# An attention and graph-convolution kernel: scores and values in double blocks, half products summed in PSUM

## The chip, the cores and the metric

The kernel runs on one core of a Trainium2 chip. The metric is the device time of one execution in microseconds (us). Before the change the median of three runs is 2770.14 us (2769.64 to 2770.96).

## What is computed

`x` is 32 batches of 512 nodes by 512 features, `adj` a 512 x 512 adjacency matrix. Two layers, each with residual and layer norm, all in float32:

```python
def _L0_gnn_ref(x, adj, Wq, bq, Wk, bk, Wv, bv):   # H, HD = 8, 64
    q = (x @ Wq + bq).reshape(b, n, H, HD)          # k, v alike
    scores = jnp.einsum('bihd,bjhd->bhij', q, k) / jnp.sqrt(jnp.float32(HD))
    mask = jnp.where(adj == 0, jnp.float32(-1000000000.0), jnp.float32(0.0))
    weights = jax.nn.softmax(scores + mask[None, None, :, :], axis=-1)
    return jnp.einsum('bhij,bjhd->bihd', weights, v).reshape(b, n, H * HD)
...
x = _layernorm(x + _L0_gnn_ref(x, adj, ...), axis=-1)
x = _layernorm(x + _L1_gnn_ref(x, adj, weight, bias), axis=-1)   # norm_adj @ (x @ weight) + bias
```

## The kernel before

All work is in `unshifted` (L50). A second function, `general`, runs only if a test at the end finds inputs out of range; it does not run here. `InOrder` (L36) records every operation of PE, DVE, ACT and POOL in program order, so each engine's queue is the order in which the code calls it, and all operations carry one line number, L44. Operations are told apart by their tiles' names.

**Products by seven.** The four matrix products with weights (values, keys, queries, and the second product of the convolution) are block products of 2 x 2 blocks done with seven multiplications instead of eight. `seven` (L309) plays them as seven pieces. A piece is four matmuls of 128 x 256 columns, each two instructions on PE, into a fresh PSUM bank; DVE, ACT and POOL add the products up in SBUF (tiles `e1`, `u1`, `u2`). `values_of` (L343) makes V, `keys_and_queries` (L368) makes K and Q for two of four head pairs, `second` in `convolve` (L710) the last product. XT, the transposed x, and the weights are held as seven half blocks, of which three are sums or differences.

**Attention.** The 8 heads go in four pairs `g`, in the order 0, 2, 1, 3; a block is one batch and one pair. `scores` (L402) computes, for two of four node tiles, keys by queries of two heads at once in the two row halves of the array (`sc`, 64 rows), DVE adds the mask (`e<-sc,maskT`), ACT takes the exponential. `accumulate` (L420) sums the exponentials on POOL, `fold` (L482) transposes and reduces these sums on DVE. `values` (L439) multiplies V by the exponentials, two heads in the two column halves of the array (`av`). `unload_values` (L456) transposes `av` on DVE into `yb`, and four DMAs on SP's queue scatter `yb` into `yT`.

**After attention.** `finish` (L532) divides by the sums, adds the residual `xr` (POOL), norms, and splits the result into two float32r parts `hi` and `lo`. `convolve` (L666) multiplies them by the adjacency (`first`, eight matmuls per tile into `zT`), then by the weights (`second`), and norms again; `store` (ACT) and a DMA put the result out.

**PSUM.** Eight banks: three pairs (`wide`), one bank `narrow`, one `av`. Pieces take wide, wide, wide, narrow in turn; scores take the pairs (L95 to L103).

**The order.** The loop at L864 goes through the 128 blocks. In one step it issues scores of block k and values of block k-1, each in halves of two tiles; in the middle part (`double`, L929) two such steps stand together, so that PE sees scores, values, scores, values, 16 instructions each, and then a share of other work: products for batch b+1, the rest of attention and the convolution for batch b-1. The shares are lists (`beside`, `side`, `cut`) written out by hand, which say after which piece of PE work each small operation of DVE, ACT and POOL is issued. `put_off` delays the POOL sums among them. The last three blocks and the end have an order of their own.

Of the kernel before, what the change touches and what calls it, by code (L numbers as in the profile page):

```python
# [49 lines left out]
def unshifted(  # L50
# [14 lines left out]

# [4 lines left out]
    G = H // 2  # L83
    SCALE = 1.0 / HD**0.5
    tensor, vector, scalar, gpsimd = (InOrder(tc, e) for e in (nc.tensor, nc.vector, nc.scalar, nc.gpsimd))
# [4 lines left out]
    small = ctx.enter_context(tc.tile_pool(name="small", bufs=3))  # L90

    psum = ctx.enter_context(tc.tile_pool(name="psum", bufs=1, space=bass.MemoryType.PSUM))
    WIDE = dict(tag="wide", bufs=3)  # L95
    turn_of = {"n": 0, "order": (WIDE, WIDE, WIDE, dict(tag="narrow"))}

    def bank(shape, tags=None):
        if tags is None:
            order = turn_of["order"]  # L100
            tags = order[turn_of["n"] % len(order)]
            turn_of["n"] += 1
        return psum.tile(shape, F32, name="mm", **tags)  # L103

    HALF = N // 2
# [3 lines left out]
    def load_x(b, j):  # L115


        if b == 1 and j == 1:
            X[b, j] = work.tile([P, 8, DT, 32], F32, name="x1", tag="e", bufs=6)
        else:  # L120
            X[b, j] = acts.tile([P, 8, DT, 32], F32, name="x", bufs=1)
        for q in range(4):
            nc.sync.dma_start(
                X[b, j][32 * q : 32 * (q + 1)],
                x[b, ts(j, HALF), ts(q, P)].rearrange("(k s) (t r) -> s k t r", s=32, r=32),
            )
# [12 lines left out]

# [9 lines left out]

# [10 lines left out]

    def combine(b, at):
        to, a, c = ((4, 2, 0), (5, 3, 4), (6, 3, 2), (2, 5, 1))[at]
        engine = gpsimd if b else vector
        engine.tensor_tensor(XT[:, to], XT[:, a], XT[:, c], ALU.subtract)
# [3 lines left out]
    def load_residual(b):  # L168

        if b < B - 2:  # L170
            t = acts.tile([P, NT, D], F32, name="xr", tag="zT", bufs=1)
            R[b] = [t[:, i, :] for i in range(NT)]
        elif b == B - 2:
            t = [acts.tile([P, 2, D], F32, name="xr2", tag=tag, bufs=n) for tag, n in (("x", 1), ("kq", 5))]
            R[b] = [t[i // 2][:, i % 2, :] for i in range(NT)]
        else:
            R[b] = [wk[:, i].rearrange("p u o -> p (u o)") for i in range(NT)]
        for i in range(NT):
            nc.sync.dma_start(R[b][i], x[b, ts(i, P), :])

# [55 lines left out]
    if B > 1:  # L236
        load_x(1, 0)
        load_x(1, 1)
# [19 lines left out]

    FINE = consts.tile([P, B + 2 * NT], F32, name="fine")
    dis = consts.tile([P, NT], F32, name="dis")  # L260

    plainT = acts.tile([P, NT, N], F32, name="plainT", tag="hi", bufs=1)

    def adjacency(m):


        p = bank([P, N])
        for n in range(NT):
            tensor.transpose(p[:, ts(n, P)], adj_sb[:, n, ts(m, P)], ident)
        vector.tensor_scalar(maskT[:, m, :], p, 0.0, FAR, op0=ALU.is_equal, op1=ALU.mult)  # L270
        scalar.copy(adjT[:, m, :], p)
        scalar.copy(plainT[:, m, :], p)

    def compare(m):

# [9 lines left out]

# [9 lines left out]

    KQ, V = {}, {}
    bias = consts.tile([P, 2, DT], F32, name="bias")
    step = consts.tile([P, 2, 2], F32, name="step")

    def biases():  # L300
        vector.tensor_copy(bias[:, 0], bk_c)
        vector.tensor_scalar(bias[:, 1], bq_c, SCALE, None, op0=ALU.mult)
        vector.tensor_sub(step, bias[:, :, 2:], bias[:, :, :2])

    def value_biases():

        vector.tensor_sub(bv_r[:, HALF:], bv_r[:, HALF:], bv_r[:, :HALF])

    def seven(multiply, first, middle, out, early=False):  # L309


        t = {}

        def piece(k, i, j):
            p = bank([P, 2, HALF])
            multiply(p, i, j)
            if k == 0:
                t["e1"] = work.tile([P, 2, HALF], F32, name="e1", bufs=1)
                first(t["e1"], p)
            elif k == 1:  # L320
                vector.tensor_add(out(0, 0), t["e1"], p)
            elif k == 2:
                t["u1"] = t["e1"]
                vector.tensor_add(t["u1"], t["e1"], p)
            elif k == 3:
                t["u2"] = work.tile([P, 2, HALF], F32, name="u2", bufs=1)
                middle(t["u2"], t["u1"], p)
                if early:
                    vector.tensor_add(out(1, 0), t["u2"], out(1, 0))
            elif k == 4:  # L330
                vector.tensor_add(out(1, 1), t["u2"], p)
                vector.tensor_add(t["u1"], t["u1"], p)
            elif k == 5 and early:
                scalar.activation(out(1, 0), p, AF.Copy, scale=-1.0)
            elif k == 5:
                vector.tensor_sub(out(1, 0), t["u2"], p)
            elif k == 6:
                vector.tensor_add(out(0, 1), t["u1"], p)

        order = [(0, 0), (1, 1), (5, 5), (6, 6), (4, 4), (3, 2), (2, 3)]  # L340
        return [(2.1, piece, (k, *order[k])) for k in ((0, 1, 5, 2, 3, 4, 6) if early else range(7))]

    def values_of(b):  # L343


        def multiply(p, i, j):
            for r in range(2):
                for u in range(2):
                    tensor.matmul(
                        p[:, r, :], XT[:, j, u, ts(r, P)], wv[:, i, u, :],  # L350
                        start=u == 0, stop=u == 1,
                    )

        def first(e1, p):
            V[b] = acts.tile([P, NT, D], F32, name="v")
            vector.tensor_add(e1, p, bv_r[:, None, :HALF].to_broadcast([P, 2, HALF]))

        def middle(u2, u1, p):
            vector.tensor_add(u2, u1, p)
            engine = gpsimd if b > 1 else vector  # L360
            engine.tensor_add(u2, u2, bv_r[:, None, HALF:].to_broadcast([P, 2, HALF]))

        def out(i, j):
            return V[b][:, 2 * j : 2 * j + 2, ts(i, HALF)]

        return seven(multiply, first, middle, out, b == 0)

    def keys_and_queries(b, r):  # L368


        def multiply(p, i, j):
            for c, w in enumerate((wk, wq)):
                for u in range(2):
                    tensor.matmul(
                        p[:, c, :], w[:, i, u, ts(r, P)], XT[:, j, u, :],
                        start=u == 0, stop=u == 1,
                    )

        def first(e1, p):
            for g in (r, r + 2):  # L380
                KQ[b, g] = acts.tile([P, 2, N], F32, name="kq", bufs=5)
            for c in range(2):
                scalar.activation(e1[:, c], p[:, c], AF.Identity, bias=bias[:, c, r : r + 1], scale=1.0)

        def middle(u2, u1, p):
            for c in range(2):
                vector.scalar_tensor_tensor(
                    u2[:, c], u1[:, c], step[:, c, r : r + 1], p[:, c], op0=ALU.add, op1=ALU.add
                )

        def out(i, j):
            return KQ[b, r + 2 * i][:, :, ts(j, HALF)]

        return seven(multiply, first, middle, out)

    def turns(b):

        return [(0, turn, (b, 0))], [(0, turn, (b, 1))] + [(0, combine, (b, k)) for k in range(4)]
# [3 lines left out]
    def scores(s, between=()):  # L402

        b, g, jj = s
        E[s] = [work.tile([P, 2, N], F32, name="e", bufs=6) for _ in range(2)]
        for l in range(2):
            j = 2 * jj + l
            e = E[s][l]
            p = psum.tile([P, 2, N], F32, name="sc", **WIDE)
# [7 lines left out]
            run(between)  # L417
            between = ()

    def accumulate(s, ls=(0, 1)):  # L420


        b, g, jj = s
        n = 2 * ORDER.index(g) + jj
        a = None
        if b == B - 1:
            if n > 1:
                t, at = ((wq, 0), (wq, 2), (wq, 4), (wk, 4), (wv, 4), (XT, 4))[n - 2]
                a = t[:, at : at + 2].rearrange("p k u o -> p k (u o)")
        if a is None and (jj == 0 or b == B - 1):  # L430
            a = work.tile([P, 2, N], F32, name="acc", bufs=2)
        if a is not None:
            ACC.setdefault((b, g), []).append(a)
            gpsimd.tensor_add(a, E[s][0], E[s][1])
        else:
            for l in ls:
                gpsimd.tensor_add(ACC[b, g][0], ACC[b, g][0], E[s][l])

    def values(s, later=False):  # L439

        b, g, jj = s
        e = E.pop(s)
        if jj == 0:
            AV[b, g] = psum.tile([P, N], F32, name="av")
        av = AV[b, g]
        for l in range(2):
            j = 2 * jj + l
            for k in range(2):
                tensor.matmul(
                    av[k * HD : (k + 1) * HD, :], V[b][:, j, ts(2 * g + k, HD)], e[l][:, k, :],  # L450
                    start=j == 0, stop=j == NT - 1,
                )
        if jj and not later:
            unload_values(b, g)

    def unload_values(b, g):  # L456
        av = AV[b, g]
        if (b, g) == blocks[-1]:
            turned = work.tile([P, N], F32, name="avT", tag="yb", bufs=1)
            scalar.copy(turned[:, :HALF], av[:, :HALF])  # L460
            vector.tensor_copy(turned[:, HALF:], av[:, HALF:])
            AV[b, g] = turned
            return

        yb = work.tile([P, 4, NT, 32], F32, name="yb", bufs=1)
# [817 lines left out]
```

## Time and profile before

| What | us |
|---|---|
| median of three runs | 2770.14 |
| the profiled execution, its own time | 2769.45 |
| its span, first to last instruction | 2767.6 |
| first matmul starts | 4.69 |
| first scores start | 50.07 |
| one batch in the middle (its pattern repeats) | 85.20 |
| last product of the tail starts | 2752.49 |

The page of the profile gives, for each engine, the time it is busy in the span: PE is the matmul engine, PEld its weight loads, which overlap, DVE the vector engine, ACT the scalar engine, POOL GpSimd, SP the queue that issues most DMAs. PEclk is the share of its clock that PE was granted. The chain of work that ended last goes back from the last instruction, at each step to what released it. Groups list instructions of one kind: how many, busy time and mean length of one, then the idle time of the engine just before them and what ended it. The timeline lists instructions by start, merged when alike. Matmuls are pipelined: a row's length covers the flight of its last matmul, so the time that a run of matmuls takes is read from its start to the start of the next.

### The profile page before, as it was taken

What the parts mean: (1) busy time and instruction counts of PE and PEld (TensorE: products, weight loads), DVE (VectorE), ACT (ScalarE), POOL (GpSimd) and SP (SyncE); (2) the same over time, 40 slices, a digit from 0 to 9 for tenths busy, and PEclk for the clock granted to TensorE, in tenths of its full rate; (3) what the DMA queues carried; (4) which work ended last, traced back from release to release, by engine and by line L of the source; (5) the groups of instructions that cost most, each with busy time, mean ns of one, the idle gap of its engine ahead of it and who ended that gap; (6) DMA issues with size and microseconds to landing.
All of it is one profiled execution on the core that took longest, in us unless ns stands there. A gap on an engine that the chain in (4) does not pass through costs nothing.

```text
span 2767.6 us, 34559 instructions
## 1 busy us (share of the span) xinstructions
PE 2744.6 (99%) x12540; PEld 1882.7 (68%) x12540; DVE 2238.2 (81%) x3199; ACT 1053.5 (38%) x1324; POOL 1786.1 (65%) x1171
## 2 busy tenths in 40 slices
PE   9999999999999999999999999999999999999997
PEld 7667676676776766767767667676676676766755
DVE  6878888788877788878888878887778887888887
ACT  2234333434334343343433343433434334343343
POOL 3666667666676666766666766667666676666666
PEclk9999999999999999999999999999999999999999
DMA  4111122111121111211112111112111121111211
GB/s 122 35 39 39 51 56 50 51 45 46 54 61 43 52 44 48 61 46 54 39 51 56 48 53 46 46 54 62 43 50 46 47 61 47 54 39 51 65 35 52
DMA packets 379108, 141.05 MB, mean 51 GB/s; under 512 B 277808, under 2 KB 345392, under 8 KB 378928
## 3 DMA queue, kind: packets, MB, share of 16 engines
q1 hardware_dynamic: 377776, 137.17, 19.1%
q8 instruction: 101, 1.65, 0.3%
q10 hardware_dynamic: 1152, 1.57, 0.2%
q14 instruction: 79, 0.65, 0.1%
HBM read 71.83 MB, written 33.55 MB: 38 GB/s over the span
## 4 chain that ended last, share of the span: by engine, by line
PE 96%; DVE 2%; POOL 1%; issue 0%; ACT 0%; DMA 0%; POOLq 0%; DVEq 0%
PE mm L44 64%; PE sc L44 17%; PE av L44 16%; POOL acc L44 0%; DVE st L44 0%; POOL xT L44 0%; DVE e L44 0%; DVE wv L44 0%; DMA xr<-in_x_dram 0%; DVE u L44 0%; DVE mv L44 0%; DVE y L44 0%; POOL yT L44 0%; DVE yT L44 0%; DVE xT L44 0%
## 5 line engine op out<-in xcount | busy, mean ns | idle before, releaser
L44 ACT ACTIVATE e<-e 128x1024 f32<-128x1024 f32 x512 | 540.7, 1057 | 719.2 <-DVE e L44 700.0
L44 DVE SCALAR_TENSOR_TENSOR e<-sc,maskT 128x1024 f32<-128x1024 f32 x512 | 605.5, 1215 | 62.7 <-PE av L44 42.1
L44 POOL TENSOR_TENSOR acc<-acc,e 128x1024 f32<-128x1024 f32 x248 | 589.0, 2375 | 89.9 <-ACT e L44 77.7
L44 POOL TENSOR_TENSOR acc<-e 128x1024 f32<-128x1024 f32 x126 | 298.6, 2370 | 331.9 <-ACT e L44 331.9
L44 PE MATMUL sc<-kq 64*128 64x512 f32 x2048 | 476.7, 603 | 0.4 <-DVE e L44 0.2
L44 PE MATMUL av<-e,v 128*64 128x512 f32 x2048 | 467.9, 599 | 0.0
L44 PE MATMUL mm<-xT,wk 128*128 128x256 f32 x1792 | 463.3, 381 | 0.0
L44 PE MATMUL mm<-xT,wq 128*128 128x256 f32 x1792 | 459.9, 379 | 0.0
L44 PE MATMUL mm<-wv,xT 128*128 128x256 f32 x1792 | 401.3, 381 | 1.9 <-issue 1.3
L44 PEld LDWEIGHTS mm<-xT,wk 128*128 128x128 f32 x1792 | 337.3, 190 | 72.1 <-DVE e L44 26.0
L44 PEld LDWEIGHTS mm<-wv,xT 128*128 128x128 f32 x1792 | 335.2, 190 | 72.4 <-DVE e L44 24.3
L44 PEld LDWEIGHTS mm<-xT,wq 128*128 128x128 f32 x1792 | 340.5, 190 | 46.3
L44 PEld LDWEIGHTS sc<-kq 64*128 64x128 f32 x2048 | 183.6, 186 | 258.3 <-DVE e L44 118.4
L44 PEld LDWEIGHTS av<-e,v 128*64 128x64 f32 x2048 | 135.4, 136 | 316.3 <-issue 269.9
L44 POOL TENSOR_TENSOR yT<-yT,xr 128x512 f32<-128x512 f32 x124 | 153.6, 1272 | 149.2 <-DVE yT L44 144.3
L44 POOL TENSOR_TENSOR yT<-yT,b_r 128x512 f32<-128x512 f32 x124 | 157.8, 1307 | 140.4 <-DVE lo L44 140.4
L44 PE MATMUL mm<-w,zT 128*128 128x256 f32 x992 | 224.6, 379 | 0.0
L44 DVE TENSOR_TENSOR e<-e,mm 128x512 f32<-128x512 f32 x224 | 153.0, 683 | 82.2 <-PE mm L44 81.9
L44 ACT ACTIVATE y<-y,add,rstd 128x512 f32<-128x512 f32 x127 | 96.1, 805 | 317.2 <-POOL add L44 317.2
L44 PEld LDWEIGHTS mm<-w,zT 128*128 128x128 f32 x992 | 188.2, 190 | 27.0 <-DVE wq L44 0.8
L44 PE MATMUL mm<-adjT,hi 128*128 128x512 f32 x496 | 200.0, 403 | 0.0
L44 PE MATMUL mm<-adjT,lo 128*128 128x512 f32 x496 | 194.4, 392 | 0.0
(144 smaller groups left out, 3212.2 us busy)
## 6 DMA issues: line engine op xcount, KB each, us to landing
out_dram<-y SPq DMA_DIRECT2D x127, 256.0 KB, 2.1
x<-in_x_dram SPq DMA_DIRECT2D x248, 128.0 KB, 2.6
yT<-yb SPq DMA_DIRECT2D x496, 64.0 KB, 2.4
xr<-in_x_dram SPq DMA_DIRECT2D x122, 256.0 KB, 3.1
wk<-in_L_gnn_Wk_dram SPq DMA_DIRECT2D x8, 128.0 KB, 5.0
wq<-in_L_gnn_Wq_dram SPq DMA_DIRECT2D x8, 128.0 KB, 4.3
yT<-in_adj_dram SPq DMA_DIRECT2D x1, 1024.0 KB, 6.0
w<-in_L_gnn_weight_dram SPq DMA_DIRECT2D x2, 512.0 KB, 7.5
```

Of the source, the lines that this page charges most:

```text
L44: return self.tc.keep_in_program_order(op(*args, **kwargs))
```

## The change

**Stretches.** `scores`, `accumulate`, `values` now take a whole block. A new `stretch` plays two blocks of scores, then POOL's sums, then two blocks of values:

```diff
+    def stretch(b, gs, gap=()):
+        for g in gs:
+            scores(b, g)
+        for g in gs:
+            accumulate(b, g)
+        av = bank([P, 2, N], "av")
+        values(b, gs[0], av[:, 0])
+        unload_values(b, gs[0], av[:, 0])
+        run(gap)
+        values(b, gs[1], av[:, 1])
+        unload_values(b, gs[1], av[:, 1])
```

A batch is: stretch of head pairs 0 and 2; fourteen products of keys and queries for batch b+1, the two chains alternating; stretch of pairs 1 and 3; then `first` of the convolution of batch b-1, the seven products of the values for batch b+1, the seven of `second`. The last batch has no products of its own between its stretches but `first`.

**PSUM.** Four pairs of banks, one tag, for everything. The two blocks' values share one pair, one block in each half.

```diff
-    WIDE = dict(tag="wide", bufs=3)
-    turn_of = {"n": 0, "order": (WIDE, WIDE, WIDE, dict(tag="narrow"))}
...
+    def bank(shape, name="mm"):
+        return psum.tile(shape, F32, name=name, tag="wide", bufs=4)
```

**Half products.** A table says for each of the seven products in which half of which pair it goes, whether it is added there to what stands in it, and where it is then moved. `put` is ACT's copy (with bias for keys and queries) and `add` a DVE add into the result; in the convolution both are DVE adds, and in batch 30 an ACT copy and a POOL add.

```diff
+    CHAIN = (
+        ("A", (0, 0), (("put", (0, 0)),)),
+        ("D", (4, 4), (("put", (1, 1)),)),
+        ("A", (5, 5), (("put", (0, 1)),)),
+        ("B", (1, 1), (("add", (0, 0)),)),
+        ("A", (6, 6), (("add", (1, 1)),)),
+        ("D", (2, 3), (("add", (0, 1)),)),
+        ("A", (3, 2), (("put", (1, 0)),)),
+    )
...
+    PLACES = dict(A=(0, 0), D=(0, 1), B=(1, 0), M=(1, 1), E=(2, 0))
+
+    def seven(table, multiply, put, add):
+        tiles, regions = {}, {}
+
+        def step(region, ij, moves):
+            fresh = region not in regions
+            if fresh:
+                n, k = PLACES[region]
+                if n not in tiles:
+                    tiles[n] = bank([P, 2, 2, HALF])
+                regions[region] = tiles[n][:, k]
+            p = regions[region]
+            multiply(p, *ij, fresh)
+            for kind, q in moves:
+                (put if kind == "put" else add)(q, p)
+
+        return each(step, *table)
```

Batch 0 uses a second table, `PLAIN_FIRST`, and the last convolution a third, `LATE_LOW`, with one region more. The bias of the values is added by POOL afterwards, four adds. `e` has eight buffers (six before), V one (two before), K and Q six (five before).

**Head and end.** `adjacency` transposes two node tiles into one pair, each half read by DVE (mask) and ACT (two copies). The values of batch 1 are no longer made among the first scores but after the second stretch of batch 0. In the end the last seven products of batch 30's convolution are played in one row beside the last batch's norm. The lists of what is issued beside which product are all new.

## The prediction

> **What bounds the kernel now.** I read the busy shares first, then the chain that ended last, then one whole batch, then single hand-overs in the timeline.
>
> ```profile
> PE 2744.6 (99%) x12540; PEld 1882.7 (68%) x12540; DVE 2238.2 (81%) x3199; ACT 1053.5 (38%) x1324; POOL 1786.1 (65%) x1171
> PEclk9999999999999999999999999999999999999999
> PE 96%; DVE 2%; POOL 1%; issue 0%; ACT 0%; DMA 0%; POOLq 0%; DVEq 0%
> ```
>
> PE is busy from end to end at full granted clock and is 96% of the chain. A busy PE could still hide stalls, so I took the windows view of one batch in the middle (the pattern repeats every 85.20 us; columns: stretch, length, busy time of PE, PEld, DVE, ACT, POOL, clock, DMA share, GB/s):
>
> ```profile
> 1000.00:1085.20 85.20, 85.20 (x388) 58.63 (x387) 69.19 (x99) 32.71 (x41) 55.77 (x37) 1.00 0.19 50
> ```
>
> PE has no idle time at all in it; DVE has 16 us to spare, ACT 52, POOL 29. So work taken from DVE (by the form rows: about 540 us of adds and copies go, 210 come back) or given to ACT (about +240) moves nothing by itself. What counts is PE's own work and any wait put in front of PE. Both programs issue the same 6796 matmuls with the same shapes.
>
> **What goes: changes of tile form.** PE's rows in the timeline:
>
> ```profile
> 1008.49 1.03 PE L44 MATMUL mm<-xT,wq 128*128 128x256 f32 x4
> 1009.45 3.70 PE L44 MATMUL sc<-kq 64*128 64x512 f32 x16
> 1013.08 3.65 PE L44 MATMUL av<-e,v 128*64 128x512 f32 x16
> 1016.67 3.70 PE L44 MATMUL sc<-kq 64*128 64x512 f32 x16
> 1020.30 3.65 PE L44 MATMUL av<-e,v 128*64 128x512 f32 x16
> 1023.88 1.13 PE L44 MATMUL mm<-xT,wk 128*128 128x256 f32 x4
> 1024.85 1.03 PE L44 MATMUL mm<-xT,wq 128*128 128x256 f32 x4
> ```
>
> Four rows of mm elsewhere follow each other at 0.865 us; here 0.96 passes before sc and 0.97 after av, 0.20 too much together. The four runs take 14.43 us where 32 pairs at 0.43 would take 13.76. So five changes of form cost 0.87 us, 0.174 each. Counted in the two built programs, PE changes form 338 times before and 201 times after (sc and av no longer alternate): 137 x 0.174 = **-23.8 us**. A stretch of two blocks is 14.1 us instead of 14.43.
>
> **What comes: waits of PE on readers.** I listed, in both built programs, every matmul that waits for an instruction issued on another engine after PE's preceding matmul; there PE can't run ahead. Before: 5. After: 327. The reason is in the built waits: two products of `seven`, A and D, lie in the two halves of one pair of banks, and the same goes for the two blocks' values in `av`. The wait is set for the whole tile: the first matmul of D (other half) waits for ACT's copy out of A, A's next product waits for the reader of D, and the second block's values wait for the transpose `yb` of the first. In a table A, D, A, B, A, D, A played without other products between, four steps wait so. For keys and queries the two heads' chains alternate, one product (1.73 us) lies between, and the wait is over in time.
>
> Price of one hand-over. A DVE reader first, in the timeline of before, where PE goes on into another bank:
>
> ```profile
> 1043.41 3.62 PE L44 MATMUL mm<-w,parts 128*128 128x256 f32 x16
> 1043.61 0.69 DVE L44 TENSOR_TENSOR y<-y,mm 128x512 f32<-128x512 f32 x1 [0.42 <-PE mm L44]
> ```
>
> The reader starts 0.20 us after PE could start the next product, and takes 0.69. Then PE's restart, one of the few places where PE waits for DVE:
>
> ```profile
> 94.09 2.35 DVE L44 SCALAR_TENSOR_TENSOR e<-sc,maskT 128x1024 f32<-128x1024 f32 x2
> 95.36 1.13 PE L44 MATMUL sc<-kq 64*128 64x512 f32 x4 [0.24 <-DVE e L44]
> 96.42 3.65 PE L44 MATMUL av<-e,v 128*64 128x512 f32 x16
> ```
>
> The first e ends at 94.09 + 1.215 = 95.31, PE starts 0.05 later, and its four matmuls then take 1.06 instead of 0.96: 0.14 in all for the restart (I use 0.05 + 0.09). The readers by form:
>
> ```profile
> L44 DVE TENSOR_TENSOR e<-e,mm 128x512 f32<-128x512 f32 x224 | 153.0, 683 | 82.2 <-PE mm L44 81.9
> L44 DVE STREAM_TRANSPOSE yb<-av 128x512 f32<-128x512 f32 x127 | 90.3, 711 | 39.5 <-DMA yT<-yb 37.4 <-PE av L44 2.1
> L44 ACT COPY zT<-mm 128x512 f32<-128x512 f32 x124 | 72.8, 587 | 259.9 <-PE mm L44 259.9
> ```
>
> DVE add: 0.20 + 0.69 + 0.14 = 1.03. ACT copy: 0.20 + 0.59 + 0.14 = 0.93. Transpose of av: 0.31 (as e after sc) + 0.71 + 0.14 = 1.16.
>
> - `av`: 64 stretches x 1.16 = 74.2.
> - Values, batches 1 to 31: per batch two ACT and two DVE hand-overs. 62 x 0.93 + 62 x 1.03 = 121.5.
> - Second product of the convolution, 30 batches, four DVE readers each: 120 x 1.03 = 123.6.
> - That makes 308 hand-overs in the steady part.
> - Head, up to the first scores (50.07 us now): values 3.9 and the first keys 2 x 1.03 + 2 x 1.13 = 4.3; the second keys 2.2; the transposes of adj, now two to a tile, wait twice for a mask (0.69) and two copies (0.59 each) of the first half, 2 x 2.2. Together 15.
> - ACT's queue in the keys stretch: `store` stands ahead of the third unload and waits for POOL's `root`. POOL starts its six sums 4.6 us after the first scores; at 2.45 each they end 19.3, which is 4.1 into the keys stretch (two blocks of scores and values with the wait on av take 15.2). `root` 1.02 + 0.2 + gaps: 5.5; `store` follows, then the unload's two activations at 0.37 and 0.47, the last done at 7.15. The fifth product, due at 4 x 1.73 = 6.91, comes 0.34 late with its restart: x 29 = 10.
> - DVE before the second stretch: `root` of the other layer is done 18.8 into the keys stretch; ACT then has four norms (0.83 + 0.63 each) and one unload (0.74) before the fourth `hi`, 25.4; DVE's last `low` (0.66) ends 26.1, and the first e, which could start at 25.7, is 0.4 late; the eighth tile of scores and av, which have 0.1 to spare, lose 0.3 together: x 30 = 9. Both queue terms are estimates from these rows laid end to end; their bounds are nought and double.
> - The mixed stretch of batch 30 and the tail, where the same waits meet a fuller DVE: 10 (0 to 25).
>
> Sum: 74.2 + 121.5 + 123.6 + 15 + 10 + 9 + 10 = 363 more, less 24: **+339 us**. A steady batch: 85.20 - 0.70 + 2.32 + 3.92 + 4.12 + 0.34 + 0.3 = 95.5 us.
>
> Costed at nothing: the first four tiles of scores find their pairs read (scores take 0.86 us a tile, e follows at 1.14, four pairs absorb eight tiles with 0.1 us to spare; that cover is what the 0.3 above eats). POOL's four adds of the bias (5.1 us) lie between the values and the next `av`, over 15 us. SP: x's second half is loaded (four DMAs, 2.6 us to landing) some 8 us ahead of its transpose; the four `yb` DMAs (2.4 us) land while the second block's values run. If the last cover went, the second transpose would be late, not PE.
>
> The Trainium skill, page "PSUM — Partial Sum Buffer", section "PSUM bank collisions raise a hardware error", asks for semaphores by bank and quadrant, not by address; by it a matmul in one half of a pair need not wait for a reader of the other, none of the 308 hand-overs of the steady part would be needed, and the sum would be about 2790. The built waits say otherwise, so the sum above stands.
>
> The Trainium skill, page "TensorE: Matmul & The Clock Gate", section "A second HAM failure mode: psum-queue depth-cycling", also speaks of this: by it, frequent short idle times in PE can halve its clock. By that page the values stretches would run at half rate and the sum would be about 4090.
>
> The nearest rows on the clock are two windows of the tail (length, PE busy, PEclk):
>
> ```profile
> 2728.00:2754.00 26.00, 23.65 (x106) 1.00 0.00 1
> 2762.00:2767.50 5.50, 0.00 (x0) 0.50 0.33 116
> ```
>
> Where PE idles 2.35 of 26 us it is granted 1.00, where it idles throughout 0.50. After, it idles some 8 of 40 us in the values stretch, between the two but much nearer to the first; I take 1.00.
>
> **The rivals.**
> 1. *The waits are over before PE comes to them*, and only the changes of form are left: 2769.45 - 24 = 2746, faster. It decides if a reader is through within 0.22 us of the last matmul's issue; the row above has 0.89. Chance 0.03 (0.01 of it with the head's cost eating the gain: no change).
> 2. *Readers queue*: ACT and DVE run in order, and folds, scales and transposes stand among the adds. If a reader comes 0.4 us late on average, 308 x 0.4 = 123 more: 3230. For it: 2.5 us of fold in front; against: by my walk the fold is through before the values. Chance 0.11.
> 3. *Hand-overs cheaper*: without the restart, and the queues' terms nought: 308 x 0.14 + 29 = 72 less: 3037; half of that still falls in the range. Chance 0.08.
> 4. *The clock falls* in the values stretches (31.6 us of PE work there): at the 0.50 of the idle row this adds up to 31 x 31.6 = 980: 4090. Against: the row with 1.00. Chance 0.03.
>
> Forecast (all hand-overs at about 1 us): chance 0.75.
>
> **The numbers.** The profiled execution took 2769.45 us (span 2767.6, 1.9 around it), the median of the three runs shown is 2770.14, 0.7 more. 2769.45 + 339 = 3108, and 0.7 for the median: 3109. Bounds: hand-overs 0.1 less and the queue terms nought, 31 + 29 less: 3049; hand-overs 0.25 more, +77, and double queues and tail up to 3195. The range takes the forecast and half of rivals 2 and 3. A measurement of this kernel tells 0.2% from no change: faster 0.02, same 0.01, slower 0.97.
>
> **What would show it.** In the profile after: PE's busy share falls to about 90%, its groups of values and second products show idle time ended by ACT `v`, DVE `v`, DVE `y`, and av by DVE `yb`; a steady batch takes 95 to 96 us; sc and av come in runs of 32. Wrong if PE's idle time is small, if the waits end on folds or on POOL, or if the granted clock is below 1.

## The result and the profile after

The changed kernel takes **3128.95 us** (median of 4, 3128.40 to 3130.41), the kernel before 2770.35 beside it: ratio 1.1295, 95% interval 1.1276 to 1.1315. It is slower by 359 us; 339 were forecast (3109). The profiled execution has a span of 3126.5 us.

From the page of the changed kernel, the lines that answer to those of before: the engines, the granted clock, the chain by engine.

```profile
PE 2822.3 (90%) x12540; PEld 1887.0 (60%) x12540; DVE 1891.6 (61%) x2685; ACT 1259.6 (40%) x1807; POOL 1789.6 (57%) x1176
PEclk9999999999999999999999999999999999999999
PE 89%; DVE 7%; issue 2%; ACT 1%; DMA 1%; SPq 0%; DVEq 0%; ACTq 0%; POOLq 0%; POOL 0%
```

PE does the same 12540 instructions and is no longer filled by them; no other engine is above 61%, so none of them is the new bound. What ends PE's idle time stands in its waits (total us, times, longest):

```profile
PE mm L44 <- DVE y L44: 107.4, 119, 2.6
PE av L44 <- DVE yb L44: 57.8, 64, 0.9
PE mm L44 <- DVE v L44: 52.5, 63, 1.4
PE mm L44 <- ACT v L44: 43.2, 64, 0.8
```

These are 310 waits of 0.7 to 0.9 us on average, 261 us together: readers of PSUM, by the names and nearly in the numbers that the prediction listed. One batch in the middle, in the windows view:

```profile
1009.25:1105.19 95.94, 87.53 (x387) 58.66 (x386) 58.65 (x82) 39.04 (x56) 55.63 (x36) 1.00 0.19 44
```

A batch takes 95.94 us instead of 85.20 (forecast 95.5). PE's rows in its timeline show the places:

```profile
1009.25 7.14 PE L44 MATMUL sc<-kq 64*128 64x512 f32 x32
1016.32 3.65 PE L44 MATMUL av<-e,v 128*64 128x512 f32 x16
1020.88 3.65 PE L44 MATMUL av<-e,v 128*64 128x512 f32 x16 [0.91 <-DVE yb L44]
...
1074.70 1.99 PE L44 MATMUL mm<-wv,xT 128*128 128x256 f32 x8 [0.68 <-ACT v L44]
1077.37 1.99 PE L44 MATMUL mm<-wv,xT 128*128 128x256 f32 x8 [0.68 <-ACT v L44]
...
1088.49 1.89 PE L44 MATMUL mm<-w,zT 128*128 128x256 f32 x8
1091.33 1.97 PE L44 MATMUL mm<-w,parts 128*128 128x256 f32 x8 [0.94 <-DVE y L44]
...
1100.43 1.99 PE L44 MATMUL mm<-w,zT 128*128 128x256 f32 x8 [0.78 <-DVE y L44]
```

A product takes 1.73 us; the one after 1088.49 starts 2.84 later. That is 1.11 more, of which only 0.94 show as idle time, since a row covers the flight of its last matmul. For the same reason PE's busy time is 78 us more for the same instructions, and the waits cost more than the 261 us of idle time. Between the two runs of values 4.56 us pass instead of 3.58. In the keys stretch, where the chains take turns, products follow each other at 1.73 with one exception of 0.08 (the product at 1031.55).

Where the 358.9 us of span lie, by the first scores of each batch in both traces: up to the first scores 50.07 became 68.75 (+18.7), batch 0 took 73.75 instead of 63.94 (+9.8), batches 1 to 29 +314.5, batches 30, 31 and the end +15.9.

### The profile page after: what moved, and what is told of

It is laid out like the page before. It is cut to its first block, busy times and chain, and to the rows that moved or that the text cites. A ratio compares the mean times of both kernels' runs of the same rounds, so it can differ in the third digit from the quotient of the medians.

```text
span 3126.5 us, 34871 instructions
## 1 busy us (share of the span) xinstructions
PE 2822.3 (90%) x12540; PEld 1887.0 (60%) x12540; DVE 1891.6 (61%) x2685; ACT 1259.6 (40%) x1807; POOL 1789.6 (57%) x1176
## 4 chain that ended last, share of the span: by engine, by line
PE 89%; DVE 7%; issue 2%; ACT 1%; DMA 1%; SPq 0%; DVEq 0%; ACTq 0%; POOLq 0%; POOL 0%
PE mm L44 59%; PE av L44 15%; PE sc L44 15%; DVE y L44 3%; DVE yb L44 1%; DVE v L44 1%; ACT v L44 1%; DMA wv<-in_L_gnn_Wv_dram 0%; DMA b_r<-in_L_gnn_bias_dram 0%; DVE wq L44 0%; DVE xT L44 0%; DVE yT L44 0%; SPq L169 0%; DVE st L44 0%; DVE kq L44 0%
## 5 line engine op out<-in xcount | busy, mean ns | idle before, releaser
L44 DVE SCALAR_TENSOR_TENSOR e<-sc,maskT 128x1024 f32<-128x1024 f32 x512 | 584.6, 1213 | 13.3 <-PE sc L44 13.3
L44 PE MATMUL mm<-wv,xT 128*128 128x256 f32 x1792 | 431.6, 387 | 95.7 <-DVE v L44 52.5
L44 PE MATMUL sc<-kq 64*128 64x512 f32 x2048 | 467.5, 601 | 4.5 <-DVE e L44 4.5
L44 PEld LDWEIGHTS av<-e,v 128*64 128x64 f32 x2048 | 156.1, 136 | 367.0 <-issue 216.9
L44 POOL TENSOR_TENSOR v<-v,bv_r 128x512 f32<-128x512 f32 x128 | 160.7, 1287 | 368.7 <-ACT v L44 362.9
L44 ACT ACTIVATE kq<-mm,bias 128x256 f32<-128x256 f32 x512 | 212.5, 466 | 254.4 <-PE mm L44 253.9
L44 PE MATMUL mm<-w,zT 128*128 128x256 f32 x992 | 240.0, 385 | 51.0 <-DVE y L44 47.9
L44 DVE STREAM_TRANSPOSE yb<-av 128x512 f32<-128x512 f32 x127 | 91.0, 716 | 271.8 <-DMA yT<-yb 232.9
L44 ACT COPY v<-mm 128x512 f32<-128x512 f32 x128 | 74.9, 585 | 375.8 <-PE mm L44 375.8
L44 DVE TENSOR_TENSOR y<-yT,mm 128x512 f32<-128x512 f32 x120 | 82.5, 687 | 236.0 <-PE mm L44 236.0
```

The lines of the kernel that those rows point to most:

```text
L44: return self.tc.keep_in_program_order(op(*args, **kwargs))
```

## The experiments

Two theories stood against each other: products wait because A and D (and two blocks' values) lie in **one tile**, or because their **readers are late** in the queues of ACT and DVE, which another place in PSUM would not mend. Kernels without a number of runs have one.

**A and D in two tiles.**

```diff
-    PLACES = dict(A=(0, 0), D=(0, 1), B=(1, 0), M=(1, 1), E=(2, 0))
+    PLACES = dict(A=(0, 0), D=(1, 0), B=(1, 1), M=(0, 1), E=(2, 0))
```

> B moves into D's pair of banks and A stands alone (A in the first tile, D and B in the two halves of the second); the products, their order and the readers stay. Theory (the waits are set for the whole tile, and A and D shared one): no product then waits for the reader of the product just before it. A steady batch of the changed kernel lost 3.93 us in the values and 4.52 in the second product against the kernel before; 31 x 3.93 + 30 x 4.5 = 257, and some 8 of the head, go: 2864 us (2850 to 2885), and the idle time ended by v and y falls from about 200 us to under 25. Rival (readers stand late in the queues of ACT and DVE, behind transposes of 1.24 us and scales of 0.6): a wait one product further back is still late, half of it stays: about 2995 us.

Measured: 2850.96 us, 278 less than the changed kernel. The waits on v are gone, and of those on y two are left:

```profile
PE mm L44 <- DVE y L44: 2.6, 2, 1.8
```

The distance from second to first scores stretch is 47.64 us instead of 56.21, and the first scores come at 55.59 instead of 68.75. The readers, their order and their engines are the same, so they were in time for any product but the very next one. The rival falls.

**Values of two blocks in two tiles.**

```diff
-        av = bank([P, 2, N], "av")
-        values(b, gs[0], av[:, 0])
+        av = [bank([P, N], "av") for _ in gs]
+        values(b, gs[0], av[0])
...
```

> The two blocks' values of a stretch go to two tiles instead of two halves of one. Theory (whole tile): the 64 waits on the transpose go; the second run of values began 4.56 us after the first instead of 3.58, so 64 x 0.97 = 62: 3067 us (3060 to 3075), the idle time ended by yb under 3 us. Rival (values of the second block are held by the transpose for another reason, its buffer or its four DMAs, 2.4 us): at most a third goes, 3108 us or more.

Measured: 3090.42 us, 38.5 less; neither theory's number. The wait on yb is gone, and the two stretches of scores and values are shorter by 1.12 and 1.10 us (14.09 instead of 15.21, 14.48 instead of 15.58, from the first scores to what follows the values). But from the first stretch to the second 39.77 us pass, hardly other than without the edit (39.73): the keys stretch between them became longer by what the first stretch had gained. PE's waits of this kernel name what came instead, a line that had 3.0 us in the changed kernel:

```profile
PE mm L44 <- ACT kq L44: 34.1, 32, 1.1
```

**Both.**

> The edits of e1_places and e2_av_tiles together. Theory (hand-overs are independent, nothing else stood behind them): the gains add, 3129 - 265 - 62 = 2802 us (2785 to 2825), PE at 98 or 99%. Rival (with the waits gone another engine or queue is late in their place, DVE before the second stretch above all): 2840 us or more.

Measured: 2783.27 us, 346 less: 29 more than the two measured gains added, and 2 under the theory's range. The rival falls. From first to second stretch 38.46 us: here the fifth product of the keys stretch, an A, waits only for A's own unload and no longer for D's, which stands behind `store` (ACT's last step of the convolution's norm, which waits for POOL's `root`). So the 34 us are not lost in this kernel.

**The step behind the missing gain.** The two tiles for values, and ACT's `store` later:

```diff
-                    0: rest + ahead["add"], 1: store[:1] + fold0, 2: store[1:2], 3: store[2:3],
-                    4: store[3:] + fold1, 5: measure[:1], 6: measure[1:2], 7: measure[2:], 8: ahead["root"],
+                    0: rest + ahead["add"], 1: fold0,
+                    4: fold1, 5: measure[:1] + store[:1], 6: measure[1:2] + store[1:2],
+                    7: measure[2:] + store[2:3], 8: ahead["root"] + store[3:],
```

> e2_av_tiles with ACT's four activations of `store` moved from behind products 1 to 4 of the keys stretch to behind products 5 to 8; nothing else moves. In e2_av_tiles the first stretch of a batch became 1.12 us shorter but the keys stretch 1.1 longer: 34.1 us of PE's idle time ended by ACT kq, which the changed kernel did not have. Theory (the unload that the fifth product needs stands behind `store`, which waits for POOL's root): that wait goes, 3090 - 34 = 3056 us (3050 to 3064). Rival (ACT or the wait on root only moves on: the norms come later, and with them DVE's last low and the scores of the second stretch): 3075 us or more.

Measured: 3054.03 us, 36.4 less than with the tiles alone; the waits on ACT kq are back at 3.0 us in 3 times, as in the changed kernel, and from the first stretch to the second 38.46 us pass. The late unload is shown to be `store`'s doing. Nothing was handed on: from the second stretch to the next first it is 55.10 us, 55.11 in the kernel with the tiles alone.

**The same wait where it was hidden.** The opposite direction: the keys' and queries' chains one after the other, so that A and D follow each other there too.

```diff
-            main = [p for pair in zip(k0, k1) for p in pair]
+            main = k0 + k1
```

> The changed kernel with the two chains of keys and queries one after the other instead of in turns; all else is the same. Theory (whole tile; turns hide the wait behind another product): 31 batches get 8 hand-overs each, 4 on ACT's two activations (0.2 + 0.37 + 0.47 + 0.1 = 1.14) and 4 on a DVE add (1.0): 31 x 8.6 = 265 more, 3395 us (3370 to 3440). Rival (the values and the second product wait because their own readers are late, not because A and D share a tile): the keys lose next to nothing, 3129 to 3145 us.

Measured: 3407.57 us, 279 more (1.12 for each of 248). The rival, next to no loss, falls. Two lines of its waits had 3.0 and 4.3 us, in 3 times each, in the changed kernel:

```profile
PE mm L44 <- ACT kq L44: 124.0, 127, 1.0
PE mm L44 <- DVE kq L44: 114.1, 127, 2.6
```

The same order with A and D in two tiles:

> e1_places (B in D's pair, A alone) with the two chains of keys and queries one after the other, as in e4_kq_in_turn. Theory (only the shared tile made the products wait): with A and D in two tiles the same order needs no hand-over, each wait lies one product (1.73 us) back; the time stays at that of e1_places, 2851 us (2845 to 2865). Rival (one chain after the other is slow by itself, since its readers can't keep up with one product per 1.73 us): the 279 us that the same step cost on the changed kernel come again, about 3130.

Measured: 2846.24 us, 5 less than with turns (one run each). The order that cost 279 us with one tile costs nothing with two. These two runs settle it: **the shared tile** is the cause.

**What is left of the gain.** With both waits gone, three late places remained in the trace; they are moved. (`low` is DVE's part in making `lo`, `lift` POOL's addition of the convolution's bias, `scale` DVE's division by the sums, `turn` the transposes of `x`.) (The new last argument of `stretch` is run behind its scores and sums; `adjacency` now turns one block, into the half of a tile that two blocks share.)

```diff
-        1: [lambda: adjacency(0)], 3: [lambda: turn(1, 0), lambda: adjacency(1)],
+        1: [lambda: adjacency(0)], 2: [lambda: adjacency(1)],
+        3: [lambda: turn(1, 0), lambda: adjacency(2)], 4: [lambda: adjacency(3)],
...
-        stretch(b, one, back["measure"][:3] if back else ())
+        stretch(b, one, back["measure"][:3] if back else (), ahead["scale"] if b == 1 else ())
...
-                    12: norm[3:] + low[2:3], 13: low[3:] + ahead["lift"],
+                    12: norm[3:] + low[2:3], 13: ahead["lift"][1:],
...
+        late = ahead["low"][3:] + ahead["lift"][:1] if 0 < b < LAST else ()
...
-                    1: fold0, 4: turn0 + fold1, 5: end["inverse"], 6: end["scale"] + bias_v + turn1,
+                    1: fold0, 3: fold1, 4: turn0, 5: end["inverse"], 6: bias_v + turn1,
```

> e3_both and three moves. The last `low` (with its lift) goes behind the scores of the second stretch: PE's scores there began 0.38 us a batch late, 11 us in all. In batch 0 the second fold goes one product ahead and the four scales behind the next scores: PE waited 2.75 us for folded and 3.08 for e there, and its clock was then 0.50 for 4 us, 1.8 more. The two blocks of adj that share a tile get a product between them: 2 waits of 2 us, and one dip of the clock to 0.57, 1.7 more. Theory (what is left beside the matmuls is these late instructions): 2783 - 11 - 7.6 - 5.5 = 2759 us (2753 to 2766), 0.35% under the kernel before. Rival (a late instruction only hands its lateness to the next one): 2770 us or more.

Measured: 2771.47 us (11 runs), ratio to before 1.0006 (0.9997 to 1.0015): 12 us less than with both, not 24. A steady batch is as expected, with PE never idle (windows view):

```profile
1017.12:1101.73 84.61, 84.61 (x388) 59.23 (x387) 61.20 (x83) 38.84 (x57) 56.33 (x36) 1.00 0.21 50
```

But the rival had its way in batch 1, where the second stretch began 51.8 us after the first (38.5 later on; 43.5 in batch 1 of the kernel with both edits). DVE's and POOL's rows there:

```profile
133.36 10.36 DVE L44 TENSOR_TENSOR yT<-yT,inv 128x512 f32<-128x512 f32 x4
143.64 0.70 DVE L44 STREAM_TRANSPOSE yb<-av 128x512 f32<-128x512 f32 x1
```

```profile
132.51 5.15 POOL L44 TENSOR_TENSOR acc<-acc,e 128x1024 f32<-128x1024 f32 x2
137.62 2.80 POOL L44 TENSOR_TENSOR acc<-e 128x1024 f32<-128x1024 f32 x1
140.49 5.43 POOL L44 TENSOR_TENSOR acc<-acc,e 128x1024 f32<-128x1024 f32 x2
```

Four scales, 0.68 each when POOL is idle, take 2.6 each beside POOL's additions of 2.4 to 2.8, and the unloads `yb` behind them hold PE, for 2.57 and 2.23 us.

**The price of a change of form**, on that kernel:

```diff
         scores(b, gs[0])
-        scores(b, gs[1])
+        scores(b, gs[1], (0, 1))
+        values(b, gs[0], av[0], (0, 1))
+        scores(b, gs[1], (2, 3))
...
```

> e8_both_dve_head with scores and values taking turns in each stretch (24 score matmuls, 8 of values, 8 of scores, 24 of values): 128 more changes of PE's tile form, and no new wait. Theory (a change of form costs 0.174 us, as the prediction's rows give it): 128 x 0.174 = 22 us over e8_both_dve_head, 0.35 us a stretch. Rival (the 0.174 was the clearing of some wait, not the change of form): within 5 us of e8_both_dve_head.

Measured: 2791.35 us, 20 more. PE's timeline, first of the kernel without, then of the one with the turns:

```profile
1063.27 7.14 PE L44 MATMUL sc<-kq 64*128 64x512 f32 x32
1070.34 7.09 PE L44 MATMUL av<-e,v 128*64 128x512 f32 x32
1077.36 0.92 PE L44 MATMUL mm<-xT,wk 128*128 128x256 f32 x3
```

```profile
1070.48 5.42 PE L44 MATMUL sc<-kq 64*128 64x512 f32 x24
1075.84 1.94 PE L44 MATMUL av<-e,v 128*64 128x512 f32 x8
1077.70 1.99 PE L44 MATMUL sc<-kq 64*128 64x512 f32 x8
1079.62 5.37 PE L44 MATMUL av<-e,v 128*64 128x512 f32 x24
1084.92 1.13 PE L44 MATMUL mm<-xT,wk 128*128 128x256 f32 x4
```

14.09 us became 14.44: 0.35 for two changes, 0.174 each, with no wait in either. The rival, within 5 us, falls.

**The version that the runs point to.**

```diff
-                    1: fold0, 3: fold1, 4: turn0, 5: end["inverse"], 6: bias_v + turn1,
+                    1: fold0, 3: turn0, 4: fold1, 6: end["inverse"] + bias_v + turn1,
...
-            vector.tensor_mul(
+            (vector if b else gpsimd).tensor_mul(
...
-        stretch(b, one, back["measure"][:3] if back else (), ahead["scale"] if b == 1 else ())
+        stretch(b, one, back["measure"][:3] if back else ())
...
+                add = ahead["add"]
+                if b == 1:
+                    scale = ahead["scale"][3:] + ahead["scale"][:3]
+                    add = [f for pair in zip(scale, add) for f in pair]
...
-    PLACES = dict(A=(0, 0), D=(1, 0), B=(1, 1), M=(0, 1), E=(2, 0))
+    PLACES = dict(A=(0, 0), D=(1, 0), B=(1, 1), M=(0, 1), F=(2, 0), E=(2, 1))
```

> e8_both_dve_head with batch 0 in another order. There DVE's four scales took 10.4 us instead of 2.7, each ending with an addition of POOL beside it; two unloads behind them came late, PE waited 4.8 us for them, 2.6 for e behind a transpose that waited for x, and its clock fell to 0.57 in between; batch 1 began its second stretch 51.8 us after the first instead of 38.5. Now batch 0's scales go to POOL, ahead of its additions; the first half of x is transposed before the second fold, and in the last batch two products of the end lie in a tile of their own. Theory (batches 0 and 1 lose their time to these late instructions): 2771.5 - 12 = 2759 us (2755 to 2764). Rival (POOL, now 5.2 us longer, is late with the sums of batch 1 and hands it on): 2767 us or more.

Measured: **2758.29 us** (5 runs), ratio to before 0.9961 (0.9947 to 0.9975). Its page has PE at 2729.0 us of a span of 2755.3; in the kernel before PE had 2744.6 of 2767.6. It is the first version here that is faster than the kernel before, by 0.4%, with an interval that lies wholly under 1. The edits were made together, so what each is worth isn't shown. A small part was handed on: in batch 1 the second stretch begins 39.8 us after the first, 1.3 more than in later batches, and PE's scores wait 1.8 us there for ACT `kq`.

**The hand-over that was dearer than forecast.**

```diff
-            engine = vector if last and at < 2 else gpsimd
+            engine = gpsimd if last and at >= 2 else vector
```

> The changed kernel with the four combinations of zT into parts on DVE instead of POOL. In its second product three of four hand-overs wait for two engines, DVE (the reader) and POOL (parts, done 15 us before); there PE started 0.15 us after the reader's end, and 0.05 after it where it waits for DVE alone. Theory (a second semaphore in the wait costs the other 0.10): all four start 0.05 after the reader, 29 x 0.3 = 9 us less: 3120 us (3117 to 3123). Rival (the 0.10 belongs to the operands, not to the second wait): the gaps stay, 3129 us, or a little more from DVE's added work.

Measured: 3142.42 us (4 runs), 13 more instead of 9 less. The gaps did what the theory said. PE and then DVE in the timeline of this kernel:

```profile
1093.34 1.89 PE L44 MATMUL mm<-w,zT 128*128 128x256 f32 x8
1096.08 1.99 PE L44 MATMUL mm<-w,parts 128*128 128x256 f32 x8 [0.85 <-DVE y L44]
```

```profile
1095.34 0.69 DVE L44 TENSOR_TENSOR y<-yT,mm 128x512 f32<-128x512 f32 x1 [2.68 <-PE mm L44]
```

The reader ends at 1096.03, PE starts 0.05 later; in the changed kernel the same pair had 0.15. The other two such places have 0.05 as well. The total was misjudged: DVE's four combinations stand ahead of its second fold, `folded` comes late, and PE waits 13.9 us in 31 times for it instead of 1.6 once; the values stretch is 0.6 us longer. The second product itself takes 16.51 us instead of 16.70, 0.19 less and not 0.30: the first product after a wait is some 0.03 us longer here.

## Why the prediction was right, step by step

The direction, the cause and the size held: 3129 lies in the range, 20 us above the forecast. Of these the head is 4, batch 0 another 4, batches 1 to 29 are 16, and the end is 4 less. The terms of a steady batch, measured as the difference between the run with the wait and the run without it:

| term | forecast us | measured us | from |
|---|---|---|---|
| changes of form | -0.70 | -0.59 | 84.61 without any wait, 85.20 before |
| two waits of `av` | 2.32 | 2.24 | 7.02 to 8.14 for 32 matmuls, twice |
| four of the values | 3.92 | 4.04 | 5.18 to 7.06, 6.91 to 9.07 |
| four of the second product | 4.12 | 4.52 | 12.18 to 16.70 |
| fifth product of the keys | 0.34 | 0.15 | 24.37 to 24.52 for the keys stretch |
| DVE late before the second stretch | 0.30 | 0.38 | 14.09 to 14.47 for the second stretch, without and with it |
| sum | 10.3 | 10.74 | 95.94 - 85.20 |

- **Changes of form**: the price of 0.174 was exact (0.35 for two). The two stretches give what was forecast: 14.43 and 14.44 us became 14.09 each. The steady batch gains 0.59 and not 0.70 because `first` gives some back: from its second matmul to its last 7.00 us pass (1064.90 to 1071.90), 6.88 in the kernel before. Why its matmuls are slower stays open.
- **Hand-overs**: `av` 1.12 (1.16 forecast), ACT 0.94 (0.93), DVE in the values 1.08 (1.03). The term mis-sized most is **the second product**: 1.13 instead of 1.03, 0.40 x 29 = 12 of the 20 us. Three of its four waits are for two engines, DVE and POOL, and such a wait ends 0.10 later; the last run shows it by taking the second engine away, and the product is then 0.19 us shorter. The other 0.21 is the 0.05 by which DVE's hand-overs in the values are dearer too. The reader starts later than in the forecast's row, where PE runs on and it is 0.20:

```profile
1090.49 0.69 DVE L44 TENSOR_TENSOR y<-yT,mm 128x512 f32<-128x512 f32 x1 [2.68 <-PE mm L44]
```

  PE could go on at 1088.49 + 1.73 = 1090.22, and the reader starts 0.27 after that.
- **ACT's queue**: forecast at 0.34, it showed 0.08 at the product itself and 0.15 in the stretch, so the rows laid end to end came out 0.2 too long. The walk counts the wait on `av` in the 15.2 us ahead of the keys stretch, which gives POOL time; with that wait gone the same queue cost 1.1 a batch. The prediction named the mechanism, but not that the wait on `av` hides most of it.
- **DVE late**: 0.38 for 0.30; moving one `low` took it away whole.
- **Range**: the upper bound, 3195, is not the sum of what stands beside it; 3109 + 77 + 19 + 15 gives 3220. The result lies under both.
- **Ends**: head 18.7 (forecast 15); batch 0 9.8, where the terms give 5.5; batches 30, 31 and the end 15.9, where they give 20.2.
- **Rivals.** 1 (waits over in time): would be 2746; the 310 waits refute it. 2 (queues): A and D in two tiles show the readers in time, its 0.4 is not there. 3 (cheaper): no kind of hand-over was under 0.94. 4 (clock): the windows 1072 to 1089 and 1089 to 1105 of the changed kernel have PE busy for 14.02 of 17 and 12.46 of 16 us, both at a granted clock of 1.00, and from 57.5 to 3050 us as a whole it is 1.00 too; it fell only in the head and the tail (0.66 from 52 to 56, 0.70 from 3058 to 3062).
- **The two pages of the Trainium skill.** The section "PSUM bank collisions raise a hardware error" of "PSUM — Partial Sum Buffer" would guard by bank and quadrant, and by it the estimate was 2790; A and D lie in different banks of the pair and waited all the same, so in this program the guard is the tile. The section "A second HAM failure mode: psum-queue depth-cycling" of "TensorE: Matmul & The Clock Gate" has frequent short idle times move the clock back and forth between half and full; the 4090 takes it at half throughout, so it is an estimate from the outer end of that. Here idle times of 0.7 to 0.9 us, repeated every 2 to 3 us, left the clock at 1.00 in both windows.

All four signs announced are there: 90%, idle time ended by ACT v and DVE v, y and yb, 95.94 us a batch, runs of 32.

## What to carry to other kernels

Before two results share a PSUM tile, list for every matmul the last instruction of another engine that it waits for: if that was issued after PE's preceding product, the whole reader (here 0.9 to 1.1 us) is paid each time; a tile of its own, or one other product in between, makes it free. And when a wait is taken out, look for the queue that it gave time to: one gain here was half eaten by ACT's `store`, and the list of waits of the new run told so.

## What the runs showed of the hardware beyond that

- In the kernel with the three moves, each of batch 0's four scales on DVE (two inputs in SBUF) ends 0.55 us after one of POOL's additions has ended: 2.6 us each on average instead of 0.68. In the kernel with both edits, mostly beside POOL's four bias additions (5.9 us), the same four took 1.16 each.
- A wait on DVE and POOL ends 0.10 us later than a wait on DVE alone: PE starts 0.15 us after the reader's end (1090.49 + 0.69 to 1091.33 in the changed kernel), against 0.05 (1095.34 + 0.69 to 1096.08 in the last run).
- The clock did fall after some single, longer idle times: to 0.50 (136 to 138 us) after 3.08 us in the kernel with both edits, to 0.62 (126 to 130) after 2.64 in the kernel with the three moves, to 0.66 (52 to 56) after 2.12 in the head of the changed kernel. It stayed at 1.00 after 2.75 in the first of these (126 to 130) and after 2.61 in the last (34 to 38), so these runs give no threshold.
